# A graph layer and a mixture of experts in one stream: two first-layer blocks per PSUM bank, result sums and ScalarE's copies put off by chunks, and a written list of steps

## The chip, the cores and the metric

The kernel runs on one core of one Trainium2 chip. The metric is device time in microseconds. The engines are TensorE (PE in the profile, its weight loads PEld), VectorE (DVE), ScalarE (ACT), GpSimd (POOL) and SyncE (SP, which issues transfers). Each works through its own queue in the order in which the program gave it the instructions.

## The reference

A node table of 6250 rows of 256 numbers goes through a graph layer and then through a mixture of eight experts, each with its own two-layer network; both add their result to the table.

```python
deg = jnp.maximum(jax.ops.segment_sum(jnp.ones(dst.shape), dst, num_segments=6250), 1.0)
norm = (deg ** -0.5)[:, None]
h = norm * (layernorm(x) @ gnn_W.T + gnn_b)
x = x + jax.ops.segment_sum(h[src], dst, num_segments=6250) * norm      # 106250 edges, dst sorted
z = layernorm(x)
scores = z @ Wg.T + bg                                                   # 8 experts
combine = softmax over the two best scores, zero elsewhere
for e in range(8):
    x_out += combine[:, e:e+1] * (relu(z @ W1[e].T + b1[e]) @ W2[e].T + b2[e])   # 256 -> 1024 -> 256
```

## The kernel before

The edges are taken in 831 chunks of 128. For a chunk GpSimd gathers 128 source rows from a table in device memory (`gather`, L389), VectorE makes a mask that says which target row each edge belongs to (`mask`, L396), and TensorE multiplies mask and rows into a running sum (`add_up`, L403). Gathers stand 6 chunks ahead in the order, and 24 row buffers hold what has landed. Several chunks that fall into one window of 128 nodes share a sum `ps`; at a window's end VectorE adds it to what came over from the window before (`join`, L478 and L481), and ScalarE copies the finished rows into the node tile they belong to (`whole`, L486).

Once all edges of a tile of 128 nodes are in (49 tiles, one about every 17 chunks), the tile is turned (L492), multiplied by the graph layer's weights (L501) and routed (`route`): second layernorm, scores, two best experts, and by a product with a matrix of slots (`sort`, L629) its rows are ordered by expert. SyncE writes them to one queue per expert in device memory (`fhq`, L641).

The experts' work goes in steps. `choose` (L653 to L689, VectorE) takes the expert with the longest queue and up to 256 rows of it; SyncE loads that expert's weights (`w1` L695, `w2` L709, 1152 and 1028 KB, three buffers each) and the rows (`xT`, L704). `up` makes the hidden layer in eight blocks of 128: two products of TensorE into a PSUM tile `ph` (L730; the profile shows each of them as two), and a Relu with bias by ScalarE (L732). `down` makes 128 result rows after another from eight products (`py`, L740), VectorE adds the bias (`y`, L744), and SyncE writes the rows to `fyq` (L746). A step has 16 pieces, 8 of `up` and 8 of `down`; a short step of 128 rows has 8 and 4.

The order is written out by hand: a loop over chunks gives out the gather, the mask and the sum of a chunk, then the tasks planned for that chunk, and then one piece of the current step (two, at every fourth chunk, if the next step is due). Steps of this stream follow the tiles: one for each tile from the fourth on, two for tiles 42, 44 and 46, 49 in all, fetched 14 chunks and started 28 chunks after a tile's last (two or three more by `LATE`). After the last chunk a second loop gives out a piece a slot, 7 further steps, the last 4 of them short, the reading of results (`read_back`, POOL, L800, and `add_in`, DVE, L808) and the storing of `out`. Which tiles' results may be read after which step is written in `DONE`; at the end the kernel looks whether that list and the queues held, and if not, runs a second, slower program (`any_order`).

In PSUM `ps`, `ph` and `py` have two tiles each, `pt` and `px` one. A tile `ph` of before holds one block, and the two take turns.

Of the kernel before, what the change touches and what calls it, by code (L numbers as in the profile page):

```python
# [7 lines left out]
F32 = mybir.dt.float32  # L8
# [11 lines left out]
P = 128  # L20
N = 6250
NT = 49
# [14 lines left out]
SLOTS = 64  # L37
FIRST_STEP = 3
EXTRA = (42, 44, 46)
FOLLOWS = [t for t in range(FIRST_STEP, NT) for _ in range(1 + (t in EXTRA))]  # L40
USUAL = len(FOLLOWS) + 7
SHORT = 4
W1C = 2 * H + HB
# [14 lines left out]

DONE = ((40, 29), (42, 33), (43, 34), (44, 35), (45, 36), (46, 38), (47, 39), (48, 40), (49, 41), (50, 42),
        (51, 44), (52, 45), (53, 46), (54, 47), (USUAL - 1, NT))  # L60
LATER = 1 << 17
# [71 lines left out]
def in_order(ctx: ExitStack, tc: tile.TileContext, g: Shared):  # L133
# [7 lines left out]

    yq = dram.tile([P + USUAL * FT, D], F32, name="fyq")

# [207 lines left out]
    for step, t1 in DONE:  # L351
        nc.vector.memset(bounds[:, t0:t1, :], float(P + (step + 1) * FT))
        t0 = t1
# [19 lines left out]
    nc.vector.memset(most, 0.0)  # L373

    zero = keep.tile([P, FT * D // P], F32, name="zero")
    nc.gpsimd.memset(zero, 0.0)  # L376

# [5 lines left out]
    def free_order(ins, others, why):  # L383
        for o in others:
            tc.declare_no_dep(ins.ins, o.ins, reason=why)
# [63 lines left out]

    def clear_results():  # L450

        for step in range(USUAL - SHORT, USUAL):
            r0 = P + step * FT + P
            nc.sync.dma_start(yq[r0:r0 + FT - P, :], zero[:, :D])

    kept = {w: (WINDOWS[w - 1][0] % P, WINDOWS[w][0] - WINDOWS[w - 1][0]) for w in range(1, len(WINDOWS))}
    keeps = {}
    for j, key in enumerate(sorted(set(kept.values()))):  # L460
        keeps[key] = keep.tile([P, 1], F32, name=f"keep{j}")
        nc.gpsimd.memset(keeps[key], 1.0)  # L462
        for t, p0, p1 in pieces(key[0], key[0] + key[1]):
            nc.gpsimd.memset(keeps[key][p0:p1, :], 0.0)
    whole, turned_sums, turned_inputs = {}, {}, {}

# [3 lines left out]
    def join(w):  # L470

        nonlocal rolled
        n0 = WINDOWS[w][0]
        n1 = WINDOWS[w + 1][0] if w + 1 < len(WINDOWS) else NP
        ps = sums.pop(w)
        new = work.tile([P, D], F32, name="rolled", bufs=3)
        if w:
            nc.vector.scalar_tensor_tensor(new, rolled, keeps[kept[w]], ps[:, 0:D], op0=OP.mult, op1=OP.add)  # L478
        else:
            nc.vector.tensor_copy(new, ps[:, 0:D])  # L480
        nc.vector.tensor_add(new, ps[:, D:2 * D], new)  # L481
        rolled = new
        for t, p0, p1 in pieces(n0, n1):
            if p0 == 0:
                whole[t] = work.tile([P, D], F32, name="whole")
            nc.scalar.activation(whole[t][p0:p1, :], new[p0:p1, :], AF.Copy)  # L486
# [158 lines left out]

    def rows_of(step):
        return P if USUAL - SHORT <= step < USUAL else FT

    def choose(step):
        n = rows_of(step)  # L650
        seen = placed
# [32 lines left out]
        to = work.tile([P, 1], F32, name="to")  # L684
        nc.vector.tensor_scalar(to, of[:, 0:1], -1.0, float(P + step * FT - LATER), op0=OP.mult, op1=OP.add)
        mine = work.tile([P, NT, 2], F32, name="mine")
# [10 lines left out]
    def load_rows(step):  # L697

        f = steps[step]
        assert sent >= f["known"]  # L700
        col = nc.values_load(f["go"][0:1, 1:2], engines=(SP,), min_val=0, max_val=CAP - FT)
        f["xT"] = work.tile([P, FT, 2], F32, name="xT", bufs=4)
        n = rows_of(step)
        nc.sync.dma_start(f["xT"][:, :n, :], hq[bass.ds(f["we"], P), bass.ds(col, n), :])  # L704
# [6 lines left out]
    def fetch(step):  # L711

        for _ in choose(step):
            yield
            if step in steps and "w1" not in steps[step]:
                load_first(step)
        while sent < steps[step]["known"]:
            yield
        load_rows(step)
        load_second(step)  # L720

    def up(step, b):
        f = steps[step]
        w1 = f["w1"]
        n = rows_of(step)
        if b == 0:
            f["hid"] = work.tile([P, HB, FT], F32, name="hid")
        ph = psp.tile([P, FT], F32, name="ph")
        for k in range(2):
            nc.tensor.matmul(ph[:, :n], w1[:, k * H + b * P:k * H + (b + 1) * P], f["xT"][:, :n, k],  # L730
                             start=(k == 0), stop=(k == 1))
        nc.scalar.activation(f["hid"][:, b, :n], ph[:, :n], AF.Relu, bias=w1[:, 2 * H + b:2 * H + b + 1])  # L732

    def down(step, i):
        f = steps[step]
        a = i // 4
        if i % 4 == 0:
            f["py"] = psp.tile([P, D], F32, name="py")
        for b in (2 * (i % 4), 2 * (i % 4) + 1):
            nc.tensor.matmul(f["py"], f["hid"][:, b, a * P:(a + 1) * P], f["w2"][:, b * D:(b + 1) * D],  # L740
                             start=(b == 0), stop=(b == HB - 1))
        if i % 4 == 3:
            y = work.tile([P, D], F32, name="y", bufs=4)
            nc.vector.tensor_add(y, f["py"], f["w2"][:, HB * D:])  # L744
            r0 = P + step * FT + a * P
            w = nc.sync.dma_start(yq[r0:r0 + P, :], y)  # L746
            free_order(w, reads, "results are written once, and read once written")
            writes.append((step, w))
        if i == 4 * rows_of(step) // P - 1:
            del steps[step]  # L750


# [16 lines left out]

    earliest = {}  # L770
    for t in range(NT):
        s = FINAL[t] + 1
        plan_at(s + 2, turn_sum, t)
        plan_at(s + 4, linear, t)
        in_parts(s + 5, route, t)
        s += LATE[t]
        for i, step in enumerate(k for k, tile in enumerate(FOLLOWS) if tile == t):
            in_parts(s + 14 + 4 * i, fetch, step)
            earliest[step] = s + 28 + 4 * i
    for w, (n0, chunks) in enumerate(WINDOWS):  # L780
        tasks.setdefault(chunks[-1] + 1, []).insert(0, (join, (w,)))
    plan_at(3, centre)
    for t in range(0, NT, 2):
        plan_at(4 + t // 2 * 3, inputs_turned, t, min(t + 2, NT))
        plan_at(6 + t // 2 * 3, inputs_scored, t, min(t + 2, NT))
    plan_at(30, clear_results)
    chosen = loaded1 = loaded2 = len(FOLLOWS)
    all_sent = FINAL[NT - 1] + 1 + 19

    cur = 0  # L790
    done = 0

# [4 lines left out]

    def read_back(pool, where, t, j, upto=USUAL - 1):
        yb = pool.tile([P, D], F32, name="yb", bufs=12)
        r = nc.gpsimd.indirect_dma_start(  # L800
            out=yb, out_offset=None, in_=yq[0:P + (upto + 1) * FT, :],
            in_offset=bass.IndirectOffsetOnAxis(ap=where[:, t, j:j + 1], axis=0))
        free_order(r, [w for step, w in writes if step > upto], "rows of later steps aren't read")
        reads.append(r)
        return t, j, yb
# [5 lines left out]
    def store(t0, t1, engine=None):  # L811
# [4 lines left out]
        if t1 == NT:  # L816
            engine.dma_start(g.out[(NT - 1) * P:N, :], g.xr[:LAST, NT - 1, :])

    def next_piece(s):

        nonlocal cur, done
        step = done
        if step >= USUAL or "xT" not in steps.get(step, {}) or s < earliest.get(step, 0):
            return
        if cur < HB:
            up(step, cur)
        else:
            down(step, cur - HB)
        cur += 1
        if cur == HB + 4 * rows_of(step) // P:  # L830
            done += 1
            cur = 0

    with tc.manual_schedule():
        with rowp as rowpool:
            for c in range(AHEAD):
                gather(c)
            for c in range(MASKS):
                mask(c)
            for s in range(NC):  # L840
                if s + AHEAD < NC:
                    gather(s + AHEAD)
                if s + MASKS < NC:
                    mask(s + MASKS)
                add_up(s)
                for fn, args in tasks.pop(s, []):
                    fn(*args)
                next_piece(s)
                if s % 4 == 0 and earliest.get(done + 1, NC) <= s:
                    next_piece(s)  # L850
        with tc.tile_pool(name="ftail", bufs=2) as pool:
# [16 lines left out]
            while done < USUAL or tasks or len(plan) > 1 or asked < 2 * allowed or pend:  # L868
                for fn, args in tasks.pop(s, []):
                    fn(*args)  # L870
                if s > all_sent:
                    if chosen < min(USUAL, done + 4):
                        run(choose(chosen))
                        chosen += 1
                    if loaded2 < min(loaded1, done + 3):
                        load_second(loaded2)
                        loaded2 += 1
# [8 lines left out]
                if len(plan) > 1 and done > plan[0][0] and s >= since.get(plan[0][0], 0) + 6 \  # L886
                        and asked == 2 * allowed:
                    step, t1 = plan.pop(0)
                    results(allowed, t1, float(P + (step + 1) * FT))
                    allowed = t1  # L890
# [10 lines left out]

            results(allowed, NT, float(P + USUAL * FT))
            late = work.tile([P, NT, 2], F32, name="late", bufs=1)
# [555 lines left out]
```

## Time and profile before

| | us |
|---|---|
| median of three runs | 1607.33 (1602.92 to 1615.76) |
| the profiled execution | 1341.47 |
| its span, first to last instruction | 1339.7 |
| PE busy | 1179.6 (88%) |
| DVE busy | 985.5 (74%) |
| POOL busy | 903.7 (67%) |
| ACT busy | 402.5 (30%) |
| mean granted TensorE clock | 0.956 |

The profiled execution is shorter than the runs; all durations below are its own. Times count from its first instruction: preparation to 82 us, then the stream over the chunks until the last sum at 1147.9 us, then the remaining steps and the reading of results. A busy TensorE is not a TensorE at its peak: the products are pipelined, and the record of each is longer than its distance to the next.

### The profile page before, as it was taken

To read this page: it belongs to the slowest core of one execution; us is meant where nothing else is said; L and a number is where in the kernel's file an instruction comes from. 1 tells how busy PE (TensorE), PEld (TensorE's weight loads), DVE (VectorE), ACT (ScalarE), POOL (GpSimd) and SP (SyncE) were. 2 spreads that over 40 slices of the span, in tenths; PEclk is the share of its full clock that TensorE was granted. 3 is DMA by queue.
4 is the path that set the end of the run, shared out by engine and by line. 5 is a ranking of instruction groups with operands and counts; after the bars stand their busy time and mean duration, and the time that the engine had idled before them with its cause. 6 is when DMAs were issued, how large, how long until landed. Compare 5 with 4: busy or idle time off the path is not lost.

```text
span 1339.7 us, 23956 instructions
## 1 busy us (share of the span) xinstructions
PE 1179.6 (88%) x6224; PEld 901.0 (67%) x6224; DVE 985.5 (74%) x5327; ACT 402.5 (30%) x931; POOL 903.7 (67%) x984
## 2 busy tenths in 40 slices
PE   4439895999899999999999999999999999889984
PEld 4417562777576677767777676776777777678873
DVE  8842657787888888888888888888877775765542
ACT  2622331232333233332323323233232222222221
POOL 2047777777777777777777777777777775347743
PEclk9999666999999999999999999999999999799987
DMA  8353456788787878788787888877978987679882
GB/s 297 112 160 104 122 138 193 227 282 272 230 250 261 274 239 286 239 268 265 251 289 228 279 258 254 288 240 270 296 229 280 296 305 236 230 235 338 313 314 89
DMA packets 158459, 326.16 MB, mean 243 GB/s; under 512 B 26708, under 2 KB 105256, under 8 KB 143976
## 3 DMA queue, kind: packets, MB, share of 16 engines
q1 hardware_dynamic: 110780, 194.17, 42.1%
q0 software_dynamic: 46864, 129.82, 33.2%
q8 instruction: 51, 0.84, 0.3%
q14 instruction: 96, 0.79, 0.2%
q10 hardware_dynamic: 668, 0.55, 0.1%
HBM read 269.01 MB, written 55.42 MB: 242 GB/s over the span
## 4 chain that ended last, share of the span: by engine, by line
PE 46%; DMA 23%; DVE 16%; issue 5%; SPq 5%; ACT 4%; POOL 2%; POOLq 0%; ACTq 0%; DVEq 0%
PE ph L730 18%; PE py L740 11%; DMA xT<-fhq 8%; PE ps L403 7%; DMA fhq<-ordered 6%; SPq L641 4%; DMA yb<-fyq,rowat 4%; DMA rows<-ftable,src 3%; PE ph L446 2%; PE pt L501 2%; PE px L629 2%; DVE mask L396 2%; DVE y L744 1%; POOL yb L800 1%; DVE rolled L481 1%
## 5 line engine op out<-in xcount | busy, mean ns | idle before, releaser
L389 POOL DMA_INDIRECT rows<-ftable,src x831 | 791.6, 953 | 253.1 <-issue 105.5
L730 PE MATMUL ph<-xT,w 128*128 128x256 f32 (+1 forms) x1792 | 472.4, 392 | 45.4 <-DMA xT<-fhq 35.7
L740 PE MATMUL py<-w,hid 128*128 128x256 f32 x1728 | 435.8, 382 | 3.9 <-DVE y L744 3.9
L730 PEld LDWEIGHTS ph<-xT,w 128*128 128x128 f32 x1792 | 322.5, 192 | 144.8 <-issue 46.6
L740 PEld LDWEIGHTS py<-w,hid 128*128 128x128 f32 x1728 | 329.8, 192 | 80.4 <-DVE y L744 4.1
L403 PE MATMUL ps<-rows,mask 128*128 128x512 f16 x831 | 318.6, 399 | 38.0 <-DMA fyq<-zero 29.9
L732 ACT ACTIVATE hid<-ph,w 128x256 f32<-128x256 f32 (+1 forms) x448 | 204.6, 465 | 291.5 <-PE ph L730 283.8
L396 DVE TENSOR_SCALAR mask<-col_b,rel 128x128 f16<-128x128 bf16 x831 | 210.0, 272 | 28.9 <-PE ps L403 28.8
L486 ACT ACTIVATE whole<-rolled 32x256 f32<-32x256 f32 (+2 forms) x156 | 64.6, 414 | 346.2 <-DVE rolled L481 345.5
L800 POOL DMA_INDIRECT yb<-fyq,rowat x98 | 94.1, 960 | 90.4 <-DVE mx L543 26.2
L403 PEld LDWEIGHTS <-mask 128*128 128x128 f16 x831 | 87.4, 105 | 67.3 <-POOL keep L462 26.1
L744 DVE TENSOR_TENSOR y<-py,w 128x256 f32<-128x256 f32 x108 | 45.4, 421 | 96.2 <-PE py L740 93.3
L478 DVE SCALAR_TENSOR_TENSOR rolled<-rolled,keep,ps 128x256 f32<-128x256 f32 x149 | 70.7, 474 | 18.0 <-PE ps L403 17.6
L808 DVE SCALAR_TENSOR_TENSOR xr<-yb,prob,xr 128x256 f32<-128x256 f32 x98 | 45.7, 482 | 50.7 <-DMA yb<-fyq,rowat 49.6
L481 DVE TENSOR_TENSOR rolled<-ps,rolled 128x256 f32<-128x256 f32 x150 | 63.6, 424 | 5.2
L501 PE MATMUL pt<-gw,uT 128*128 128x264 f32 x196 | 55.9, 411 | 2.0 <-DVE spot L595 2.0
L509 DVE SCALAR_TENSOR_TENSOR xr<-pt,norm,xr 128x256 f32<-128x256 f32 x49 | 23.7, 483 | 41.7 <-PE pt L501 41.5
L446 PEld LDWEIGHTS ph<-wg,turned 128*128 128x128 f32 x196 | 38.6, 289 | 16.8 <-ACT turned L438 16.1
L199 PE MATMUL count<-oh,ol 128*16 128x8 bf16 (+2 forms) x898 | 28.9, 174 | 22.2 <-DVE oh L188 17.9
L501 PEld LDWEIGHTS pt<-gw,uT 128*128 128x128 f32 x196 | 39.4, 203 | 13.5 <-DVE spot L595 2.1
L376 POOL MEMSET zero<- 128x512 f32 x1 | 0.5, 524 | 64.5 <-DMA ftable<-tab 64.5
L199 PEld LDWEIGHTS <-ol 128*16 128x16 bf16 x898 | 28.7, 109 | 22.5 <-DVE ol L185 16.2
(188 smaller groups left out, 1144.6 us busy)
## 6 DMA issues: line engine op xcount, KB each, us to landing
w<-in_W SPq DMA_DIRECT2D x56, 1152.0 KB
w<-in_W SPq DMA_DIRECT2D x56, 1028.0 KB
fhq<-ordered SPq DMA_DIRECT2D x392, 64.0 KB
fyq<-y SPq DMA_DIRECT2D x108, 128.0 KB
xT<-fhq SPq DMA_DIRECT2D x52, 256.0 KB
rows<-ftable,src POOLq DMA_INDIRECT x831
out<-xr POOLq DMA_DIRECT2D x11, 512.0 KB
xr<-in_x SPq DMA_DIRECT2D x6, 896.0 KB
```

Source lines behind the costliest of these rows:

```text
L389: nc.gpsimd.indirect_dma_start(out=rows[c], out_offset=None, in_=table[:, :], in_offset=bass.IndirectOffsetOnAxis(ap=g.src[:, c:c + 1], ax ...
L396: nc.vector.tensor_scalar(masks[c], g.col_b[:, r:r + P], g.rel[:, c:c + 1], None, op0=OP.is_equal)
L403: nc.tensor.matmul(sums[w], masks.pop(c), rows.pop(c), start=(c == chunks[0]), stop=(c == chunks[-1]))
L446: nc.tensor.matmul(px, xT[:, k, (t - t0) * P:(t - t0 + 1) * P], wg[:, k, :], start=(k == 0), stop=(k == 1))
L478: nc.vector.scalar_tensor_tensor(new, rolled, keeps[kept[w]], ps[:, 0:D], op0=OP.mult, op1=OP.add)
L481: nc.vector.tensor_add(new, ps[:, D:2 * D], new)
L486: nc.scalar.activation(whole[t][p0:p1, :], new[p0:p1, :], AF.Copy)
L501: nc.tensor.matmul(pl, uT[:, k, :], gw[:, k, :], start=(k == 0), stop=(k == 1))
L730: nc.tensor.matmul(ph[:, :n], w1[:, k * H + b * P:k * H + (b + 1) * P], f["xT"][:, :n, k], start=(k == 0), stop=(k == 1))
L732: nc.scalar.activation(f["hid"][:, b, :n], ph[:, :n], AF.Relu, bias=w1[:, 2 * H + b:2 * H + b + 1])
L740: nc.tensor.matmul(f["py"], f["hid"][:, b, a * P:(a + 1) * P], f["w2"][:, b * D:(b + 1) * D], start=(b == 0), stop=(b == HB - 1))
L800: r = nc.gpsimd.indirect_dma_start(out=yb, out_offset=None, in_=yq[0:P + (upto + 1) * FT, :], in_offset=bass.IndirectOffsetOnAxis(ap=where ...
```

## The change

- `ph` becomes one tile for two blocks: block b writes half b % 2 of it, and a new tile is taken at every even block.
- `join` is split. The sum stays at the chunk after the window's end; ScalarE's copies (`part_of`) come `BEHIND` = 2 chunks later, and all that is planned for a tile (`turn_sum`, `linear`, `route`) comes 2 chunks later too.
- `down` leaves the adding of the bias and the write of the result to a task of the next slot (`leave`), which also counts the steps that are gone; second weights are loaded when a step is less than 3 ahead of that count.
- The steps are a list (`STREAM`): six of 128 rows from chunk 75 on, then 42 of 256 at written chunks, each started 14 chunks after its entry at the earliest and only with its second weights issued; then `TAIL`, five of 256 and six of 128. 59 steps in place of 56. `DONE` is a new list for them.
- Pieces are given out by credit: each chunk adds 1250 less 222 and less what the tile work planned for that chunk takes by a table, up to 2000; a piece takes 600 to 915.
- The clearing of the second halves of short steps' results is left out, since a step has as many result rows as it has rows.

```diff
-FIRST_STEP = 3
-EXTRA = (42, 44, 46)
-FOLLOWS = [t for t in range(FIRST_STEP, NT) for _ in range(1 + (t in EXTRA))]
-USUAL = len(FOLLOWS) + 7
-SHORT = 4
+STREAM = ((75, 128), (84, 128), (93, 128), (102, 128), (111, 128), (120, 128), (142, 256), (159, 256),
...
+          (720, 256), (738, 256), (755, 256), (772, 256), (789, 256), (804, 256), (819, 256), (834, 256))
+TAIL = (256, 256, 256, 256, 256, 128, 128, 128, 128, 128, 128)
+ROWS_OF = [n for s, n in STREAM] + list(TAIL)
+USUAL = len(ROWS_OF)
+START = [P + sum(ROWS_OF[:step]) for step in range(USUAL + 1)]
+LEAD = 14
+BEHIND = 2
+SLOT = 1250
+CHUNK = 222
+SPARE = 2000
+TASKS = dict(turn_sum=220, linear=890, rank=100, sort=430, inputs_turned=800, inputs_scored=1570)
+PIECES = {FT: (915, 870), P: (600, 870)}
...
-        (51, 44), (52, 45), (53, 46), (54, 47), (USUAL - 1, NT))
+        (50, 38), (51, 40), (52, 41), (53, 42), (54, 43), (55, 44), (56, 45), (57, 46), (USUAL - 1, NT))
...
-    zero = keep.tile([P, FT * D // P], F32, name="zero")
-    nc.gpsimd.memset(zero, 0.0)
...
         rolled = new
+        summed[w] = new
+
+    def part_of(w):
+        n0 = WINDOWS[w][0]
+        n1 = WINDOWS[w + 1][0] if w + 1 < len(WINDOWS) else NP
+        new = summed.pop(w)
         for t, p0, p1 in pieces(n0, n1):
...
         for _ in choose(step):
             yield
-            if step in steps and "w1" not in steps[step]:
+            if step in steps and "w1" not in steps[step] and step < done + (cur >= HB) + 3:
                 load_first(step)
+        while "w1" not in steps[step]:
+            if step < done + (cur >= HB) + 3:
+                load_first(step)
+            else:
+                yield
         while sent < steps[step]["known"]:
             yield
         load_rows(step)
+        while step >= gone + 3:
+            yield
         load_second(step)
...
-        ph = psp.tile([P, FT], F32, name="ph")
+        if b % 2 == 0:
+            f["ph"] = psp.tile([P, 2, FT], F32, name="ph")
+        ph = f["ph"][:, b % 2]
...
         if i % 4 == 3:
-            y = work.tile([P, D], F32, name="y", bufs=4)
-            nc.vector.tensor_add(y, f["py"], f["w2"][:, HB * D:])
-            r0 = P + step * FT + a * P
-            w = nc.sync.dma_start(yq[r0:r0 + P, :], y)
-            free_order(w, reads, "results are written once, and read once written")
-            writes.append((step, w))
+            plan_at(s + 1, leave, step, a, f["py"], f["w2"])
...
-        s = FINAL[t] + 1
+        s = FINAL[t] + 1 + BEHIND
...
     for w, (n0, chunks) in enumerate(WINDOWS):
         tasks.setdefault(chunks[-1] + 1, []).insert(0, (join, (w,)))
+        plan_at(chunks[-1] + 1 + BEHIND, part_of, w)
...
-    plan_at(30, clear_results)
+    for step, (s, n) in enumerate(STREAM):
+        in_parts(s, fetch, step)
+        earliest[step] = s + LEAD
...
+    def ready(s):
+        return done < USUAL and "w2" in steps.get(done, {}) and s >= earliest.get(done, 0)
...
-                next_piece(s)
-                if s % 4 == 0 and earliest.get(done + 1, NC) <= s:
+                credit = min(credit + SLOT - CHUNK - busy.get(s, 0), SPARE)
+                while credit > 0 and ready(s):
+                    credit -= PIECES[ROWS_OF[done]][cur >= HB]
                     next_piece(s)
...
-                if s > all_sent:
+                if s > all_sent and s > max(STREAM)[0] + 6:
...
-                    if loaded2 < min(loaded1, done + 3):
+                    if loaded2 < min(loaded1, gone + 3):
```

## The prediction

> **What bounds the kernel now.** I read the table of engines by stretch first, then the lines of single instructions, the waits of TensorE, and the timeline.
>
> ```profile
> 600.00:700.00 100.00, 97.45 (x457) 72.81 (x454) 85.40 (x476) 32.28 (x76) 75.93 (x80) 1.00 0.83 264
> ...
> 1148.00:1182.00 34.00, 23.97 (x90) 18.44 (x89) 28.12 (x173) 6.63 (x16) 14.18 (x15) 0.78 0.76 271
> ```
>
> After the stretch and its length stand busy us (and instructions) of PE, PEld, DVE, ACT and POOL, then TensorE's clock, the transfers' share and GB/s. In a steady stretch TensorE looks full, and POOL does 80 gathers in 100 us. Two lines of instructions say who sets the pace (min/median/max ns, first to last start in us):
>
> ```profile
> L389 POOL DMA_INDIRECT rows<-ftable,src x831: 942/946/1189, 82.0 to 1127.3; - x167
> ...
> L403 PE MATMUL ps<-rows,mask x831: 376/379/634, 86.8 to 1147.9; 128*128 128x512 f16 x167
> ```
>
> (1127.3 - 82.0) / 830 is 1.26 us for a gather: 0.95 of work and about 0.30 that stand before nearly every one, whoever is named as releaser. POOL never waits longer, so up to 1127.3 us the gathers set the pace. The last sum is 20.6 us behind the last gather, where the first was 4.8: TensorE falls behind late.
>
> ```profile
> PE ph L730 <- DMA xT<-fhq: 35.7, 27, 7.9
> ...
> PE ph L730 <- ACT hid L732: 8.7, 11, 1.9
> ```
>
> These are TensorE's waits (us, times, longest): on ScalarE's Relu it hardly waits. After the stream TensorE is the bound, as the timeline of a tail step shows, with ScalarE's Relus beside it:
>
> ```profile
> 1269.12 7.37 PE L730 MATMUL ph<-xT,w 128*128 128x256 f32 x32
> 1276.33 7.07 PE L740 MATMUL py<-w,hid 128*128 128x256 f32 x32
> ```
>
> ```profile
> 1270.27 0.47 ACT L732 ACTIVATE hid<-ph,w 128x256 f32<-128x256 f32 x1 [7.38 <-PE ph L730]
> 1271.12 0.47 ACT L732 ACTIVATE hid<-ph,w 128x256 f32<-128x256 f32 x1 [0.38 <-PE ph L730]
> 1272.02 0.47 ACT L732 ACTIVATE hid<-ph,w 128x256 f32<-128x256 f32 x1 [0.43 <-PE ph L730]
> ```
>
> A step of 256 rows is 7.2 us up and 6.9 down, nothing between: 14.1. A block of the first layer is four products 0.226 apart, 0.90 us; its Relu comes while the next block runs.
>
> [...]
>
> **The change, part by part.**
>
> Two blocks in one ph. In the changed instruction list the first product of every odd block waits for the Relu of the even block just before it[...]; in the list of before a block waits for the Relu two blocks back. That is 4 waits a step, 236 in all. Price: a Relu that finds ScalarE free starts 0.42 us after the start of its block's fourth product (median of 316 in the trace; the first one above, at 1270.27 for products from 1269.12 on, gives 0.47) and takes 0.47; TensorE resumes about 0.05 later, and its first product after a wait takes 0.1 more than 0.226. That is 1.04 against 0.226: 0.81 us lost where nothing stands between. For blocks of 128 rows the Relu takes 0.37:
>
> ```profile
> 1306.72 0.98 PEld L730 LDWEIGHTS ph<-xT,w 128*128 128x128 f32 x8 [0.25 <-ACT hid L732]
> 1307.47 0.82 ACT L732 ACTIVATE hid<-ph,w 128x128 f32<-128x128 f32 x2 [0.41 <-PE ph L730]
> 1307.89 0.98 PEld L730 LDWEIGHTS ph<-xT,w 128*128 128x128 f32 x8 [0.20 <-ACT hid L732]
> ```
>
> Two blocks now take 1.17 us (1306.72 to 1307.89), with a wait in them; in a row with a Relu each they would take about 1.8, so 0.62 a pair. What the list puts between a pair shortens its loss: a sum's product 0.215, the four of a sort 0.43.
> - Stream, 184 pairs: of those of 256 rows 44 have nothing between, 57 one sum's product (0.59 left), 54 about 0.65 us of work (0.16 left), the other 5 little; of 128 rows 16 nothing, 7 one product (0.4). 35.6 + 33.6 + 8.6 + 0.8 + 12.7 = 91 us, 2.0 a step.
> - Tail, 52 pairs, all but one with nothing between: 28 x 0.81 + 24 x 0.62 = 37.6 us.
>
> In the stream there is a cover. A tile comes every 17 gathers, 21.3 us. For it TensorE has 14.1 of the step, 17 x 0.215 of sums, 0.89 of L501, 0.43 of L629, 0.22 of L492: 19.3. The wait of 2.0 fills the rest, and a Relu queued behind another ScalarE operation adds (I take 0.4): 21.7 against 21.3, so over 40 steps TensorE falls back 16 us. Behind the waiting product stand the sums' products, and for those POOL waits once the 24 row buffers are full, 30 us behind. This cover is gone in the tail.
>
> Fewer rows, paced. 59 steps hold 13,568 rows, 56 held 13,824: 14.1 us less for TensorE, all of it in the stream, since at chunk 831 the lists leave 186 pieces against 178: 7 full and 6 short steps against 8 and 4, which at 14.1 and 8.0 us (from one first block at 1305.60 to the next at 1313.54 in the timeline) is 146.7 against 144.8. The last 31 chunks hold a fifth less of such work than before, so that the lateness of 20.6 us there need not come. From 5 us at the first sum, 16 by the waits and up to 10 carried from the six short early steps: 21 to 31. I take the last sum 5 us later than before; bounds -13 (waits hidden) and +20.
>
> Queues and transfers. Three more steps cost VectorE three times about 3.7 us of choose (L653 to L689), beside 985 busy of 1340; SP three pairs of weight issues, 2.2 MB each, against four clears of 128 KB less; POOL nothing. The first six steps ask 2.2 MB each within 51 chunks (64 us): 204 GB/s, and 105 for the gathers, 309, where the page's best slice is 338. Late weights there delay early steps only, which the gathers cover; nothing to 5 us, counted in the 10 above. POOL's memset of zero (0.52 us before the first gather) goes: -0.5.
>
> Copies two chunks later, y one slot later. They take waits from the heads of ScalarE's and VectorE's queues (y L744 after py: 93.3 us of idleness). Behind them stand Relus and masks, but TensorE waits for the Relus only 8.7 us in all, its weight loads 25.5; worth 0 to 9, taken as 0, since the Relu's delay is in my 0.4. Each tile is routed two chunks later: at the end 1.7 us, inside the next term.
>
> Tail's start and end. Choosing resumes at slot 854, and only 12 pieces (10 us, 13 with waits) are left before step 48, which needs 3.7 of choosing and about 10 of weights and rows: 2 us late, bounds 0 to 6. In 1148 to 1182 TensorE waits for the last tile's route about 12 us anyway, and this swallows about 5 of the new waits. Last, three tiles' rows are read after the last step, not two: two gathers, +2.5.
>
> Sum: 5 - 0.5 + 37.6 - 5 + 1.9 + 2 + 2.5 = +43.5 us on the profiled execution's 1341.5 (span 1339.7, 1.8 around it): 1385, 3.2% more. The median of the runs is 1607.3, 266 us above that execution, and no view shows why. I carry the ratio: 1660.
>
> **Rivals.**
> - TensorE is slower in the runs, and the bound in the stream too (its clock there averages below the 19.3/21.3 = 0.91 at which the gathers stop leading). For: 266 us are missing somewhere and the page shows half-clock windows. Against: 0.96 in the profiled execution. All waits then count: about 80 + 38 + 6 of ends, less the 14.1 us saved at a clock of 0.8 (18): +106, 1713.
> - The weight loads count: 6.5 MB at the page's 243 GB/s are 27 us, and the waits hide under them: 1634. For: a share of 0.98 in one tail stretch. Against: gathers wait for nothing and TensorE only 6.6 us for rows.
> - Not slower: the runs are bound by TensorE's work, and the new wait falls into time it loses anyway. Then 18 us are saved, 4 given back at the ends: 1593. It decides only where a pair costs under 0.1 us (22 us over 236 pairs), against 0.8 here. For: in the stream half the pairs have work between. Against: the tail.
> - The list misjudges the queues and the second program at the end runs: many times slower. The reference's inputs, put through the rule of choose, leave no row behind and end with two empty steps; 1 in 100.
>
> **How the numbers follow.** The forecast (1635 to 1690) 0.55; slower TensorE 0.20; transfers 0.08; the not-slower rival 0.16, half of it more than 1% down; the last 0.01. 1% is about what a measurement of this kernel can tell. The range 1600 to 1725 takes in both bounds of the stream and of the tail and the next two cases. Slower 0.84, same 0.08, faster 0.08.
>
> **What would show it.** TensorE's wait for the Relu becomes its largest, some 200 times at 0.3 to 0.8 us. A full tail step's 32 first-layer products take about 10.5 us, not 7.2. The last sum starts at 1135 to 1168. From there to the end it is about 231 us, not 192. I am wrong if those products still take 7.2 us, or if the tail is as long as before; wrong in size if the gathers show gaps over 0.3 us, for then the stream is TensorE's.

## The result, and the profile after

The changed kernel takes 1702.30 us (median of 4 runs, 1697.25 to 1704.19) against 1611.55 us (4 runs, 1602.92 to 1619.67): a ratio of 1.056 [1.049, 1.063], slower. That is above the forecast of 1635 to 1690 and inside the wide range of 1600 to 1725. The profiled execution of before, 1341.47 us, on which the prediction's sum stands, was never seen again: no other execution of that kernel, in all sets together, was below 1578 us. So the changed profile is set here beside one of the unchanged kernel in a later set, called *before in the runs* (1590.94 us, span 1589.2). In that set the kernel before ran at 1587.80 us, 23.75 us below its 1611.55 beside the changed kernel, so a part of each difference between these two profiles belongs to the sets and not to the change.

The two groups of lines on gathers and sums, first before in the runs, then after (min/median/max ns, first to last start in us):

```profile
L389 POOL DMA_INDIRECT rows<-ftable,src x831: 940/946/1186, 82.0 to 1337.8; - x167
...
L403 PE MATMUL ps<-rows,mask x831: 376/379/634, 86.6 to 1371.3; 128*128 128x512 f16 x167
```

```profile
L400 POOL DMA_INDIRECT rows<-ftable,src x831: 940/946/1180, 82.1 to 1432.1; - x167
...
L414 PE MATMUL ps<-rows,mask x831: 376/379/634, 85.8 to 1464.4; 128*128 128x512 f16 x167
```

The steady stretch that the prediction showed, before in the runs and then after, with the same columns:

```profile
600.00:700.00 100.00, 87.35 (x379) 63.19 (x378) 71.91 (x400) 27.19 (x64) 63.84 (x68) 0.95 0.68 215
```

```profile
600.00:700.00 100.00, 79.04 (x332) 56.95 (x333) 64.07 (x358) 25.50 (x59) 58.14 (x62) 0.91 0.60 186
```

Of 80 gathers and 97 us of busy TensorE in the 1341 us execution 68 and 87 are left in the runs of before, 62 and 79 after. A gather and a sum's product last as long as in the 1341 us execution (medians of 946 and 379 ns). Only the distances have grown: 1.26 us from gather to gather there, (1337.8 - 82.0) / 830 = 1.51 in the runs of before, 1.63 after. The last sum starts 93.1 us later than before in the runs, and from there to the end of the span it is 237.1 us against 217.9. Who holds the gathers is in POOL's waits (us in total, times, longest), before in the runs and after:

```profile
POOL rows L389 <- issue: 184.5, 560, 3.3
POOL rows L389 <- PE ps L403: 164.1, 148, 3.5
```

```profile
POOL rows L400 <- PE ps L414: 275.4, 177, 9.9
POOL rows L400 <- issue: 169.3, 527, 1.2
```

In the 1341 us execution the wait for sums was never over 0.3 us; here it reaches 3.5 and 9.9 us. The gathers wait for row buffers that TensorE's sums have not given back, so TensorE, with the waits in its queue, holds up the stream, in the runs of before already. (Its products stand in the program's order: the 1723 changes of the tile they write in the 1341 us execution, and the 1511 in the changed kernel's profile, are those of the instruction list.) TensorE's own waits, again before in the runs and then after:

```profile
PE ph L730 <- issue: 55.7, 47, 3.6
PE ph L730 <- ACT hid L732: 54.9, 28, 3.7
```

```profile
PE ph L746 <- ACT hid L748: 154.3, 109, 8.4
PE ph L746 <- issue: 68.4, 61, 6.5
```

The wait ahead of first-layer products goes from 110.6 us to 222.7 under these two names, and from 128.8 to 251.4 under all. ("issue" names no releaser; of the tail steps that follow the one below, some have it where the others have the Relu. The trace of the 1341 us execution holds 33,244 updates of semaphores, the signals between engines; the later ones hold 11,393 to 15,376, so more of their waits have no name or the wrong one.) The timeline of a full tail step of the changed kernel, TensorE and then ScalarE in the same stretch (start, length, instructions, idle before):

```profile
1563.53 1.06 PE L746 MATMUL ph<-xT,w 128*128 128x256 f32 x4
1565.21 2.08 PE L746 MATMUL ph<-xT,w 128*128 128x256 f32 x8 [0.61 <-ACT hid L748]
1567.86 2.08 PE L746 MATMUL ph<-xT,w 128*128 128x256 f32 x8 [0.56 <-ACT hid L748]
1570.50 2.08 PE L746 MATMUL ph<-xT,w 128*128 128x256 f32 x8 [0.56 <-ACT hid L748]
1573.14 1.17 PE L746 MATMUL ph<-xT,w 128*128 128x256 f32 x4 [0.56 <-ACT hid L748]
1574.15 7.07 PE L756 MATMUL py<-w,hid 128*128 128x256 f32 x32
```

```profile
1564.69 0.47 ACT L748 ACTIVATE hid<-ph,w 128x256 f32<-128x256 f32 x1 [7.38 <-issue]
1566.42 0.47 ACT L748 ACTIVATE hid<-ph,w 128x256 f32<-128x256 f32 x1 [1.26 <-PE ph L746]
1567.33 0.47 ACT L748 ACTIVATE hid<-ph,w 128x256 f32<-128x256 f32 x1 [0.43 <-PE ph L746]
```

TensorE issues four products, stops until the even block's Relu is through (1564.69 + 0.47 = 1565.16, and TensorE goes on at 1565.21), and then issues eight. One pair is 1567.86 - 1565.21 = 2.65 us where two blocks of four products at 0.226 from start to start (the record of each is 0.39) are 1.81: 0.84 lost. The step takes 10.62 us up, not 7.2.

The same part of the program before in the runs shows what the 1341 us execution had not:

```profile
1469.28 7.37 PE L730 MATMUL ph<-xT,w 128*128 128x256 f32 x32
...
1483.40 1.97 PE L730 MATMUL ph<-xT,w 128*128 128x256 f32 x8
1488.33 7.30 PE L730 MATMUL ph<-xT,w 128*128 128x256 f32 x24 [2.96 <-issue]
1495.46 7.07 PE L740 MATMUL py<-w,hid 128*128 128x256 f32 x32
```

```profile
1487.80 0.47 ACT L732 ACTIVATE hid<-ph,w 128x256 f32<-128x256 f32 x1 [10.63 <-remote]
1488.53 0.47 ACT L732 ACTIVATE hid<-ph,w 128x256 f32<-128x256 f32 x1 [0.26 <-remote]
```

The step at 1469.28 runs as in the 1341 us execution. In the next one TensorE has done the first two blocks by 1485.4, ScalarE has been idle for 10 us, and yet the Relu of the first block starts only at 1487.80. With both `ph` tiles full TensorE stands still meanwhile, for 2.96 us. The Relu's go-ahead came some 3 us late ("remote": no product had ended shortly before the signal).

### The profile page after: what moved, and what is told of

Read it like the earlier page. It is cut to its first block, busy times and chain, and to the rows that moved or that the text cites. A ratio compares the mean times of both kernels' runs of the same rounds, so it can differ in the third digit from the quotient of the medians.

```text
span 1701.5 us, 24224 instructions
## 1 busy us (share of the span) xinstructions
PE 1273.4 (75%) x6288; PEld 934.6 (55%) x6288; DVE 1004.2 (59%) x5402; ACT 409.6 (24%) x955; POOL 902.2 (53%) x983
## 4 chain that ended last, share of the span: by engine, by line
PE 57%; DVE 14%; issue 12%; another core or an unknown queue 7%; ACT 6%; DMA 2%; SPq 1%; POOL 0%; ACTq 0%; POOLq 0%; DVEq 0%
PE ph L746 26%; PE py L756 13%; PE ps L414 9%; ACT hid L748 4%; PE pt L511 3%; PE ph L457 2%; DVE mask L407 2%; PE px L639 1%; DMA xT<-fhq 1%; DVE y L768 1%; PE px L446 1%; DVE rolled L481 1%; DVE rs L542 1%; PE count L213 1%
## 5 line engine op out<-in xcount | busy, mean ns | idle before, releaser
L746 PE MATMUL ph<-xT,w 128*128 128x256 f32 (+1 forms) x1888 | 537.0, 418 | 253.5 <-ACT hid L748 154.3
L746 PEld LDWEIGHTS ph<-xT,w 128*128 128x128 f32 x1888 | 358.8, 213 | 415.0 <-ACT hid L748 212.4
L756 PE MATMUL py<-w,hid 128*128 128x256 f32 x1696 | 418.2, 380 | 0.0
L756 PEld LDWEIGHTS py<-w,hid 128*128 128x128 f32 x1696 | 320.2, 190 | 67.0 <-issue 0.5
L748 ACT ACTIVATE hid<-ph,w 128x256 f32<-128x256 f32 (+1 forms) x472 | 213.0, 452 | 583.1 <-PE ph L746 321.0
L414 PE MATMUL ps<-rows,mask 128*128 128x512 f16 x831 | 315.0, 410 | 50.7 <-DMA rows<-ftable,src 31.4
L457 PE MATMUL ph<-wg,turned 128*128 128x8 f32 x196 | 41.6, 340 | 32.9 <-ACT turned L449 32.9
L836 DVE SCALAR_TENSOR_TENSOR xr<-yb,prob,xr 128x256 f32<-128x256 f32 x98 | 45.4, 481 | 17.7 <-DMA yb<-fyq,rowat 16.3
L574 ACT ACTIVATE ex<-ex 128x1 f32<-128x1 f32 x49 | 9.9, 202 | 174.7 <-DVE ex L573 35.2
```

What stands on the lines that cost most here:

```text
L414: nc.tensor.matmul(sums[w], masks.pop(c), rows.pop(c), start=(c == chunks[0]), stop=(c == chunks[-1]))
L457: nc.tensor.matmul(px, xT[:, k, (t - t0) * P:(t - t0 + 1) * P], wg[:, k, :], start=(k == 0), stop=(k == 1))
```

## The experiments

There are five sets: the result above and four more, each of these on a chip of its own, and each beside its own runs of the kernel before. That kernel's median was 1611.55 (the result above), 1587.80, 1609.08, 1590.02 and 1589.95 us, so ratios of one set are compared first. The ratios are those on record; they are not the quotients of the two medians beside them, from which they differ by up to 0.4%, so that a step of 1% may be read a few tenths larger or smaller. In the names, "two blocks per bank" is two blocks in one tile `ph`, "one block" a tile for each.

| kernel | before, us | this, us | ratio | last sum starts | from there to the end |
|---|---|---|---|---|---|
| changed | 1611.55 | 1702.30 | 1.056 [1.049, 1.063] | 1464.4 | 237.1 |
| before again | 1587.80 | 1590.96 | 1.002 [0.999, 1.004] | 1371.3 | 217.9 |
| before, two blocks per bank | 1587.80 | 1679.34 | 1.060 [1.056, 1.065] | 1443.2 | 234.2 |
| changed, one block per bank | 1587.80 | 1610.49 | 1.018 [1.014, 1.023] | 1392.0 | 216.7 |
| changed, copies at the window's end | 1587.80 | 1667.39 | 1.053 [1.050, 1.057] | 1424.3 | 235.1 |
| changed, one block, old pacing | 1609.08 | 1609.74 | 1.000 [0.997, 1.002] | 1391.9 | 213.1 |
| before, tile work 2 chunks later | 1609.08 | 1614.82 | 1.004 [1.001, 1.007] | 1387.5 | 225.4 |
| before, layers interleaved | 1609.08 | 1592.95 | 0.988 [0.985, 0.991] | 1376.0 | 221.1 |
| changed again | 1590.02 | 1659.86 | 1.042 [1.037, 1.047] | 1427.3 | 237.5 |
| changed, one block per bank, again | 1590.02 | 1616.64 | 1.015 [1.010, 1.020] | 1395.3 | 222.5 |
| changed, one block, old pacing, again | 1590.02 | 1591.92 | 1.003 [1.001, 1.006] | 1370.3 | 211.5 |
| before, two blocks per bank, again | 1590.02 | 1677.46 | 1.055 [1.051, 1.059] | 1435.9 | 233.5 |
| changed, old pacing | 1589.95 | 1629.93 | 1.026 [1.018, 1.034] | 1395.0 | 228.0 |

The last two columns are from each kernel's one profiled execution.

### Before, unchanged

> The kernel before, unchanged, to see which of its two times (1341 us in the profiled execution, 1603 to 1620 in the runs) a second profile shows, and where the 266 us between them lie. If the gap is a slower TensorE clock, the granted clock is near 0.8 and the products are farther apart. If it is late signals, the products keep 0.226 us and the waits of TensorE and ScalarE grow. Ratio to before 1.00 either way.

1.002 [0.999, 1.004], with no execution near 1341 us. The base of the prediction's sum was an exception. Profiling as such did not shorten an execution here: this run's profiled one took 1590.94 us, the median of its 20 runs 1590.96. Why the first took 1341 us stays open; its trace was also recorded differently, with 33,244 semaphore updates against 12,308 here.

Where the time lies can be told. The span is 249.5 us longer. TensorE's busy time grows from 1179.6 to 1259.9 us, and its idle time (stops of over 0.15 us) from 143.2 to 311.5. So about two thirds are waits and one third is a slower TensorE: the trace has the clock at half for 275.8 us against 120.4, and half of those 155.4 us gives an estimate of 78 for the 80 us of longer work, if TensorE worked all through them. (Medians in the 1341 us execution: first-layer products of 256 rows that follow each other are 0.427 us apart at half clock and 0.226 at full.) Both of the expectation's cases hold in part, with a mean clock of 0.914 and not 0.8.

### Bank sharing alone, and everything but bank sharing

```diff
 # before, two blocks per bank (the one edit)
-        ph = psp.tile([P, FT], F32, name="ph")
+        if b % 2 == 0:
+            f["ph"] = psp.tile([P, 2, FT], F32, name="ph")
+        ph = f["ph"][:, b % 2]
```

> The kernel before with two blocks per bank and nothing else of the change. If the wait for the even block's Relu is the cost: 1.05 to 1.08 of before, since here one piece a chunk leaves less of it uncovered in the stream but the tail has all of it. If the rest of the change is the cost: 0.99 to 1.01.

The changed kernel with one block per bank is the same edit the other way round.

> The changed kernel with one block per bank again, all else as changed. If the wait of an odd block for the even block's Relu is the cost, the time falls by nearly the whole loss, to 0.97 to 1.01 of before. If list, credit and postponed copies cost the time, it stays at 1.04 to 1.06.

Sharing alone makes the kernel before 6.0% slower; the changed kernel without it is 1.8% slower than before. Compared with before in the runs, sharing moves the last sum from 1371.3 to 1443.2 us and lengthens the tail by 16.3 us: most of the loss lies in the stream. TensorE's waits in the shared version of before:

```profile
PE ph L732 <- ACT hid L734: 177.8, 152, 6.9
PE ph L732 <- ACT whole L486: 39.2, 10, 4.9
```

against 54.9 us in 28 waits for the Relu before in the runs. The two ratios multiply to 1.080 where the whole change gave 1.056, so either the sets differ or the parts don't add; that called for the later sets.

### ScalarE's copies back at the window's end

```diff
-        plan_at(chunks[-1] + 1 + BEHIND, part_of, w)
+        tasks[chunks[-1] + 1].insert(1, (part_of, (w,)))
```

> The changed kernel with ScalarE's copies at the window's end again, tiles still two chunks later. If the late copies matter little, as the prediction has it, the ratio to before stays at 1.05 to 1.065; if they keep Relus from standing behind a wait for VectorE, it rises to 1.07 or more; if they hurt, it falls below 1.04.

1.053 [1.050, 1.057]. The changed kernel itself was not in this set. It gave 1.056 in one set and 1.042 in another: what the copies' delay is worth under shared banks lies between -0.3% and +1.1% and stays open.

### The old pacing in place of the credit, and tile work put off in the kernel before

```diff
 # changed, one block, old pacing: beside the bank edit
-                credit = min(credit + SLOT - CHUNK - busy.get(s, 0), SPARE)
-                while credit > 0 and ready(s):
-                    credit -= PIECES[ROWS_OF[done]][cur >= HB]
+                next_piece(s)
+                if s % 4 == 0 and earliest.get(done + 1, NC) <= s:
                     next_piece(s)
```

> The changed kernel with one first-layer block per bank again, and with the pacing of the kernel before in place of the credit: one piece a chunk, a second at every fourth chunk when the next step is due. One block per bank alone gave 1.018 of the kernel before. Theory A (what is left of the 1.8% is the credit, which issues pieces in pairs with nothing between a product and the Relu it needs): 1.000 to 1.008. Theory B (it is the later tile work and the new list of steps): 1.013 to 1.022, no different from the run with the credit. TensorE's waits for the first layer's Relu should fall from 55 us under A and stay under B.

```diff
 # before, tile work 2 chunks later (join split as in the change)
-        s = FINAL[t] + 1
+        s = FINAL[t] + 1 + BEHIND
...
+        plan_at(chunks[-1] + 1 + BEHIND, part_of, w)
...
-    all_sent = FINAL[NT - 1] + 1 + 19
+    all_sent = FINAL[NT - 1] + 1 + 19 + BEHIND
```

> The kernel before, with ScalarE's copies and all of the tile work behind them two chunks later; bank use, pacing, sizes of steps and their number as before. Theory A (postponing costs only what the last sum's tile work gains in time at the end, two chunks of about 1.3 us, as the sum of the prediction has it): 1.000 to 1.005. Theory B (postponing is what is left of the change's time once the banks are single): 1.012 to 1.020. A gain, 0.985 to 0.998, if the copies at the window's end held up sums on TensorE in the stream, as the words of the change have it.

Postponing costs 0.4% [0.1, 0.7], inside what theory A gave it. With one block per bank and the old pacing the changed kernel equals before (1.000), which speaks for the credit as the rest. The waits for the Relu did not clearly follow: under its name they fell, to 29.7 us, but with 86.1 of "issue" that is 115.8, where the credit's run, in another set, had 54.6 and 65.9, 120.5. What did fall is the wait for a step's rows (`xT`): 4.0 us against 25.2 with the credit.

### The layers of two steps interleaved

```diff
-        if cur < HB:
-            up(step, cur)
+        if can_up and (turn == 0 or not can_down):
+            up(ups, cur)
+            cur += 1
+            turn = 1
...
-            down(step, cur - HB)
+            down(done, low)
+            low += 1
+            turn = 0
```

A piece of a step's first layer takes turns with one of the second layer of the step ahead (`ups` counts first layers, `done` second ones); weights are loaded by those counts.

> The kernel before with the first layer of a step issued piece by piece in turn with the second layer of the step ahead of it, so that each Relu has twice as many products between it and the next use of its bank; the same products, Relus and banks. In the run of the kernel before TensorE waits 111 us for the first layer's Relus (55.7 + 54.9), and in the kernel with two blocks per bank some 180. Theory A (TensorE's waits on Relus that come late set the pace of the stream, not the gathers): these waits fall to under 40 us, and the time by 40 to 90 us: 0.94 to 0.975. Theory B (the gathers set the pace, and TensorE's waits in the stream lie under them): only the tail gains, 0.98 to 1.0.

0.988 [0.985, 0.991]: 1.2% below the kernel before and the best ratio found, but that is 16 us, not 40 to 90. TensorE's waits, of this kernel:

```profile
PE px L629 <- DVE slots L607: 47.6, 16, 5.9
PE px L629 <- DVE slots L606: 34.6, 12, 4.5
...
PE ph L732 <- ACT hid L734: 14.0, 7, 4.8
```

With "issue" (29.4) the waits ahead of first-layer products fall from 110.6 to 43.4 us, nearly as theory A wanted. But the product that sorts a tile, which waited 18.1 us for VectorE's `slots` before in the runs (11.7 + 6.4), now waits 82.2. Theory A misses in the time. Theory B's number is met, but not its reason, so far as it can be told: the set has no profile of before, and beside its two other kernels the last sum comes 11.5 and 15.9 us earlier while the tail lies between theirs. All of TensorE's stops over the span come to 337.3 us, where the other two kernels of the set have 334.6 and 344.5, though ahead of first-layer products this one has 58.8 (under all names) and they have 119.8 and 149.3. So most of what the first layer is spared is waited elsewhere.

### The change and its parts on one chip

> The changed kernel as it is, beside its own variants and two blocks per bank alone, so that all four stand against the same runs of the kernel before; in the runs so far the kernel before itself stood at 1588 in one set and at 1609 to 1612 in the others. Theory A (the parts add up, and the set explains why 1.018 and 1.060 did not make 1.056): the ratio is 1.06 to 1.08 in a set where the kernel before runs at 1588, 1.050 to 1.062 where it runs at 1610. Theory B (the kernel's ratio is the same in every set, 1.050 to 1.062, and the parts overlap).

> The changed kernel with one first-layer block per bank, again. Theory A (the credit costs): 1.012 to 1.022, and slower than the same kernel with the pacing of before by 1% or more. Theory B (the 1.018 stood beside a faster set of the kernel before; the list, the postponed work and the credit are worth nothing that can be measured): within 0.7% of the kernel with the pacing of before, and both at 1.000 to 1.008 if the kernel before is at 1610 again.

> The same with the pacing of the kernel before, again. Theory A (the credit costs): 0.997 to 1.003. Theory B (the credit is worth nothing): within 0.7% of the kernel with the credit, whatever that is.

> The kernel before with two first-layer blocks per bank and nothing else, again. Theory A (bank sharing is nearly the whole of the change): within 0.8% of the changed kernel in the same set. Theory B (the rest of the change gives back a part of what sharing costs, or adds to it): more than 0.8% away from it.

The same changed program gave 1.042 [1.037, 1.047] here, in the fourth set, and 1.056 [1.049, 1.063] in the first: both theories on the sets fall. The granted clock was 0.89 to 0.90 in the four runs there and 0.910 on average here; that is 1.7% at most of a 2.6% longer time, and what else differed isn't known.

Inside this set the steps are clear: old pacing and one block 1591.92, with the credit 1616.64 (+24.7 us), with shared banks too 1659.86 (+43.2). The credit costs in the stream (last sum 1370.3 to 1395.3) and in the tail (+11.0); sharing costs 32.0 in the stream and 15.0 in the tail (the spans of the profiled executions differ by 36.0 and 47.0 us where the medians give 24.7 and 43.2, and these splits are theirs). Theory A on the credit holds. TensorE's waits ahead of first-layer products, one block, first old pacing, then credit:

```profile
PE ph L744 <- issue: 79.4, 49, 5.1
...
PE ph L744 <- ACT hid L746: 28.9, 14, 4.4
```

```profile
PE ph L744 <- issue: 88.0, 62, 4.5
PE ph L744 <- ACT hid L746: 51.3, 17, 6.7
```

Here they rise by 31.0 us, in step with the 24.7. The traces show where the pacings differ. Of the 322 later blocks of steps in the stream, 3 follow the block before them with no other product between under the old pacing, and 107 under the credit. TensorE stops for 76.3 us ahead of those 107. All stops ahead of later blocks grow from 92.4 to 119.0 us, and those ahead of a step's first block from 7.3 to 23.4. In the same pair from the second and third sets, the first sum hardly grew (100.3 to 103.5) and the second did (4.0 to 33.2). It fits that the credit gives out two pieces in one chunk, so that a Relu has less other work to hide behind, but that was no whole account in either pair, and no run tries it alone.

Two blocks on the kernel before cost 87.4 us, twice what they cost on the changed one, and end 17.6 us above the whole change: theory B of the last expectation here.

### Sharing with the old pacing

The credit's edit above, on the changed kernel with its shared banks.

> The changed kernel with two blocks per bank and all its other parts, but with the pacing of the kernel before (one piece a chunk, a second at every fourth chunk when the next step is due) in place of the credit: the fourth of the combinations of banks and pacing with the new list, of which the others gave 1.003 (one block, old pacing), 1.015 (one block, credit) and 1.042 to 1.056 (two blocks, credit). Theory A (costs of sharing and of the credit are separate and add up): sharing is worth 2.7 to 4%, so 1.028 to 1.043, below the changed kernel. Theory B (they do not add up: under shared banks the credit gives back part of what sharing costs, since with one piece a chunk nearly every pair is cut by a chunk and each chunk waits for one Relu): 1.050 to 1.063, as two blocks alone on the kernel before, which gave 1.055 and 1.060.

1.026 [1.018, 1.034]: below the changed kernel, as theory A has it, and just under the 1.028 to 1.043 that it named. So on the new list sharing costs 2.3% with the old pacing and 2.6% with the credit, and the credit costs 1.5% with shared banks and 1.2% without (two of these four are taken across sets): the two add up, within intervals of 0.2 to 0.8%. Of the 4.2% that the change cost in the fourth set, about 2.5 are the shared bank, 1.3 the credit, and 0.3 all the rest. The 5.6% of the first set is not taken apart.

Why sharing costs the kernel before 5.5 to 6.0% is settled only as to the place. There TensorE stops for 116.2 us (112.3 in the second run) ahead of blocks of the stream that have products of a tile's work between them and the block before, all of it at the second block of a pair; before in the runs it is 18.7 us, in the kernel of this section 64.0, in the changed kernel of the fourth set 16.2. Of the 116.2 us 37.5 stand under the name of ScalarE's copies (`whole`), which the changed kernel has 2 chunks later. The changed kernel with its copies put back has 3.8 us under that name and was at most 1.1% slower, but it has the credit too. Old pacing, shared banks and copies at the window's end were not run together on the new list.

## Why the prediction was right, and where it was not

- **The sign and the mechanism** were right. The Relu wait is TensorE's largest, in 170 waits; they average 1.31 us, above the 0.3 to 0.8 given. But 110.6 us of such waits stood in the runs of before already, in 75 waits, where the 1341 us execution had 8.7 us in 11. Why a block should wait for the Relu of the other half of its tile, no trace or run here shows. The wait stands in the changed instruction list, and the changed trace has its cost: a stop of 0.56 us inside a pair of the tail although the two blocks lie in different halves. No run shows what comes without it.
- **The price of a pair** was right where it is clean: 0.84 us in the tail step for 0.81 predicted, and 10.62 us for the step's first layer for "about 10.5". For 128 rows it was too high: two blocks at 1624.37 and 1626.00 are 1.63 us apart, 0.46 over the 1.17 of before, where 0.62 was taken.
- **"Tail, 37.6 us"** was mis-sized. Sharing alone measured 16.3 us (two blocks on before) and 15.0 (on the changed kernel). The tail it was added to, 192 us, was that of the 1341 us execution; in the runs of before it is 217.9, where late Relus stop TensorE already (the step at 1483.40 takes 12.1 us up). Ahead of first-layer products TensorE stops in the tail for 0 us in the 1341 us execution, 17.9 before in the runs and 39.4 after; 39.4 is close to the 37.6 predicted, but the 17.9 were there before the change. The end itself, "about 231 us, not 192", was nearly met at 237.1, by luck: from a different start, by a smaller step.
- **"In the stream there is a cover"** is the step that failed. The 91 us were to hide under gathers 1.26 us apart, and the last sum was to come 5 us later (bounds -13 and +20). It came 93.1 us later, and 56.0 in the fourth set, both beside the profile of before from the second. In the runs the gathers are 1.51 us apart before the change and wait for TensorE, so what stops TensorE mostly lengthens the stream. Where the sum had 16 us for the waits, sharing measured 32.0 on the changed kernel and 71.9 on the kernel before. The prediction's own sign for this, gathers with gaps over 0.3 us, is what the profile shows, and its first rival, TensorE bound in the stream, 1713, came closest to 1702. The rival's reason was only half right: not a lower clock alone (0.914 before in the runs, above its 0.91), but waits. And its sum was met in part by luck: it had 80 us for pairs in the stream and none for the credit.
- **"Fewer rows, paced"** priced the credit by the pieces left at the last chunk (+1.9) and the work saved, and never by what pieces given out together do to TensorE's waits. The credit measured +24.7 us by the medians of the fourth set, 1.2% by the ratios.
- **"Copies two chunks later, y one slot later", taken as 0**, and the rest: +0.4% for postponing alone; 0.0 and +0.3% for all the change but banks and credit. That was right within what could be told.
- **The carried ratio**, 3.2%, made 1660. Measured were 5.6% in the first set and 4.2% in the fourth, where the median happens to be 1659.86. That agreement is luck and not the sum's merit: its tail was too dear and its stream too cheap.
- **The rival "not slower"** wanted pairs at under 0.1 us; its thought, that the new wait falls into time lost anyway, held for over half of the tail's cost (15.0 to 16.3 us came of 37.6).

## What to carry to other kernels

In this program TensorE's filling of one first-layer block overlapped ScalarE's emptying of the one before only while the two lay in different `ph` tiles: in the tail step at 1469.28 TensorE ran 32 products without a stop. Putting two blocks in one tile turned this rotation into a stop of 0.56 us for each pair, 0.84 us lost, where nothing stood between. Before a wait is called hidden, check that the profiled execution takes as long as the runs: the cover that is 2 us wide in the 1341 us execution was gone in every later profile. And look at what a scheme that evens out busy time by issuing pieces in pairs does to the distance between a product and the result it needs: here the credit put 107 blocks where 3 had been, directly behind the block before, and cost 1.2 to 1.5%, in part perhaps for that reason.

## What the runs showed of the hardware

The late signals were not expected. I take every Relu that found ScalarE free (its last instruction over at most 0.3 us after the block's fourth product had started) and count those that start over 0.2 us after the recorded end of that product, where 0.04 is usual: none of 332 in the 1341 us execution, 27 of 257 before in the runs, 63 of 236 with the layers interleaved, 38 of 397 in the second profile of the changed kernel. (By the start of the fourth product, with 0.42 usual and over 0.6 called late, there would be 9, 68, 80 and 86; but 9, 41, 17 and 49 of these are products that took 0.52 to 0.63 us in place of 0.39, all but two of them at half clock, and their Relus followed at once.) Of the 27, 19 are over 1 us late and the longest is 4.3.

It is the signal that is late, and not ScalarE. Where a Relu comes in time, the update of TensorE's semaphore is recorded 0.01 us after the product's end and the Relu starts 0.02 us after that. For 21 of the 27 an update is recorded too, and the Relu starts as soon after it, 0.01 to 0.04 us; the update itself is late. (By the profile's own note ends of products are modelled, but for 25 of the 27 the next product had started by then as usual.) In the tail step shown above the second block's fourth product ends at 1485.37, its update is recorded at 1488.51, and the Relu starts at 1488.53. Whether TensorE goes on or stops does not decide it: 25 of 210 are late where it goes straight on and 2 of 47 where it stops, before in the runs, but 23 of 265 and 12 of 129 in the first profile of the changed kernel. What holds the signals up, and why one execution had none of it, these runs do not tell.
